# One attention head's scores at a later place among the block products, query transposes ahead of the output projection, and one query chunk in another PSUM bank

## The chip, the cores and the metric

The kernel runs on one core of one Trainium2 chip. The time is the device time of one execution in microseconds (us), taken as the median of several runs. All data are 32-bit floats.

## The reference, cut to what matters

The reference is a cross-attention with two kinds of context rows. There are 8 batches. Each has 112 query rows of 320 channels (`x`) and 375 context rows of 512 channels; the last 4 of those are "prompt" rows and the other 371 are "text" rows. There are 20 heads of 16 channels.

```
q = x @ W_q ; k = text @ W_k ; v = text @ W_v          (per head)
p = softmax(q k^T / 4)                                  112 x 371 per head
text_out = p v
qsem = l2norm(p @ text)                                 112 x 512 per head
fused = q k_ip^T / 4 + 0.5 * qsem @ l2norm(prompts)^T   112 x 4 per head
out = (text_out + softmax(fused) * mask @ v_ip) @ W_out + b_out + x
```

The norm of `p @ text` is the costly part. The kernel never forms the 512 wide product: with G = text text^T (371 x 371, the same for all heads of a batch) the squared norm of a row is p G p^T, so one product of `p` with the triangle of G, a multiplication by `p` and a sum give it. The columns for `p v`, the row sum of `p` and the prompt products are set beside G, so that one chain of matmuls yields all of them.

## The kernel before, in words

**Tiling.** A batch `b` is worked in five steps `g` = 0 to 4 of four heads `a` = 0 to 3 each, so there are 40 steps (b, g). One head lies on 32 of the 128 partitions: head `a` of a step uses partitions 32a to 32a+31. I call these 32 rows of TensorE's array **strip a**. Four matmuls on four strips can be under way together.

**Products of a step** (`multiplied`, L510 to L531). A step has 12 blocks `j` of 32 context rows. In each block every head has one matmul (L523) from its strip: the transposed probabilities of that block against the rows of G and of the values in the tile `u`. Only the upper triangle is multiplied, so the blocks get narrower: 392 columns in block 0, 360 in block 1, and so on by 32 down to 40 in block 11. Each head adds up in a PSUM bank of its own (`ps_qd`, four banks). A matmul of 32-bit floats is two passes in the trace, each with a weight load and a matmul record: 40 steps x 48 matmuls x 2 = 3840 records on L523.

**Scores** (`scores`, L476). While a step's products run, the scores of the step two ahead (`LEAD = 2`) are made for its four heads: one matmul of 371 columns each, on strip `a`, between the blocks. A score goes to one of the two banks of the pool `ps_sc`, taken in turn. `probabilities` then takes the row maximum on VectorE (L489), the exponential on ScalarE (L493), and issues on SyncE's queue the DMA that lays the probabilities of the head out for the transposition (L496). The main loop sets the places by hand:

```
at = {0: (0, 1), 4: (2, 3)}.get(j, ())
```

After block 0 come the scores of heads 0 and 1, after block 4 those of heads 2 and 3. As there are two banks, head 2's score needs head 0's exponential to be done, and head 3's needs head 1's. After block 2 VectorE transposes the coming step's probabilities (`transposed`, L504).

**After the blocks of a step** come `reduced` (ScalarE copies L536, VectorE multiply and sum L538), the GpSimd copies of the next step's values into `u` (`placed`, L445), and then in `between` (L665) the projections of the next batch: `gram` (L362) in step 0, `values` (L409) and `keys` (L393) in steps 1 to 3, and in step 4 the transposes of the context of batch b+2 (`transposed_context`, L339, copies L349), the output projection of batch b-1 (fourth piece of `finish`, L633, with its addition L640 on VectorE) and, in steps (1, 4), (3, 4) and (5, 4) alone, the queries of the coming batches (`project_queries`, L269): two batches at a time, but one in (5, 4).

**`project_queries`** has six pieces: three transposes of chunks of `x` (L281, copied by ScalarE, L284) and three chunks of `x W_q` (L289), each read by VectorE (L298, two readings, or one for the last chunk) and by ScalarE (L301) after VectorE.

**PSUM banks.** `ps_qd` has four, `ps_sc` two, and `ps_mm` two for everything else. `bank(name, spare=True)` takes a bank of `ps_sc` in place of one of `ps_mm`. Before the change these use it: the third chunk of the context (`ps_c`, b > 1), the output projection `ps_o` (all but the last batch), and the first transposed chunk of `x` (`ps_x`).

**Order.** The instructions of TensorE, SyncE and VectorE run in the order in which the program emits them; ScalarE's and GpSimd's are set by the framework's scheduler.

Of the kernel before, what the change touches and what calls it, by code (L numbers as in the profile page):

```python
# [20 lines left out]
def kernel(  # L21
# [58 lines left out]
    def bank(name, spare=False):  # L80

        if spare:
            return ps_sc.tile([P, 512], F32, tag="sc", name=name)
        return ps_mm.tile([P, 512], F32, tag="mm", name=name)
# [21 lines left out]
    FULL = C // P  # L106
# [162 lines left out]
    def project_queries(bs):  # L269
        n = len(bs)  # L270
        xT = work.tile([P, NC, 2 * S], F32, tag="xT", name=f"xT_{bs[0]}", bufs=1)
        qT = work.tile([P, NC, 2 * S], F32, tag="qT", name=f"qT_{bs[0]}", bufs=2)
        qm = work.tile([P, NC, 2, 2 * S], F32, tag="qm", name=f"qm_{bs[0]}", bufs=2)
        for j, b in enumerate(bs):
            queries[b] = (qT, qm, j)
        nc.gpsimd.memset(xT[REST:, FULL, :], 0.0)
        for i in range(NC):
            cn = min(P, C - i * P)
            ps = bank(f"ps_x_{bs[0]}_{i}", spare=bs[0] > 1 and i == 0)
            for j, b in enumerate(bs):  # L280
                nc.tensor.transpose(  # L281
                    ps[:cn, j * S : (j + 1) * S], x_sb[:, b, i * P : i * P + cn], ident[:S, :S]
                )
            nc.scalar.copy(xT[:cn, i, : n * S], ps[:cn, : n * S])  # L284
            yield
        for i in range(NC):
            ps = bank(f"ps_q_{bs[0]}_{i}")
            for j in range(NC):
                nc.tensor.matmul(  # L289
                    ps[:, : n * S],  # L290
                    wq_sb[:, j, i * P : (i + 1) * P],
                    xT[:, j, : n * S],
                    start=(j == 0),
                    stop=(j == NC - 1),
                )

            for r in range(2 if i < FULL else 1):
                nc.vector.tensor_scalar_mul(  # L298
                    qm[:, i, r, : n * S], ps[:, : n * S], emask[:, r : r + 1]
                )  # L300
            nc.scalar.copy(qT[:, i, : n * S], ps[:, : n * S])  # L301
            yield
# [8 lines left out]
    def begin(b):  # L311
        s = st[b] = dict(ct=loaded.pop(b))
        s["ctxT"] = work.tile([P, NE, TP], F32, tag="ctxT", name=f"ctxT_{b}")
        nc.gpsimd.memset(s["ctxT"][:, :, T:], 0.0)
        s["kT"] = work.tile([P, NC, TT], F32, tag="kT", name=f"kT_{b}")
        s["ud"] = dram.tile([P, GCOL[NT]], F32, tag="ud", name=f"ud_{b}")
        s["vext"] = work.tile([P, NT, GROUP, NG, D], F32, tag="vext", name=f"vext_{b}", bufs=1)
        s["vd"] = dram.tile([TP, C], F32, tag="vd", name=f"vd_{b}")
        s["u"] = work.tile([P, UCOL], F32, tag="u", name=f"u_{b}")
        s["vr"] = work.tile([P, BLK, NG, D], F32, tag="vr", name=f"vr_{b}")  # L320
        s["ipl"] = work.tile([S, H, NIP], F32, tag="ipl", name=f"ipl_{b}")
        s["ss"] = work.tile([S, H], F32, tag="ss", name=f"ss_{b}")
        s["pvs"] = work.tile([S, H, VW], F32, tag="pvs", name=f"pvs_{b}")
        s["vip"] = work.tile([S, NIP, H, D], F32, tag="vipb", name=f"vip_{b}")
# [6 lines left out]
    def transposed_context(b):  # L331
        begin(b)
        s = st[b]
        ct, ctxT = s["ct"], s["ctxT"]
        for c in range(NT):
            rows = min(P, TT - c * P)
            ps = bank(f"ps_c_{b}_{c}", spare=b > 1 and c == 2)
            for e in range(NE):
                nc.tensor.transpose(  # L339
                    ps[:, e * P : e * P + rows],  # L340
                    ct[:rows, c, e * P : (e + 1) * P],
                    ident[:rows, :rows],
                )
            o = ctxT[:, :, c * P : c * P + rows]
            i = ps.rearrange("p (e t) -> p e t", t=P)[:, :, :rows]
            if c % 2 and b < 1:
                nc.vector.tensor_copy(o, i)
            else:
                nc.scalar.copy(o, i)  # L349
            yield  # L350

    def gram(b):

        ctxT = st[b]["ctxT"]

        nc.gpsimd.tensor_copy(ctxT[:, :, TT:T], ipnT[:, :, b * NIP : (b + 1) * NIP])
        for c in range(NT):
            t0 = c * P
            k = min(P, TT - t0)
            ps = bank(f"ps_g_{b}_{c}")  # L360
            for e in range(NE):
                nc.tensor.matmul(  # L362
                    ps[:, : T - t0],
                    ctxT[:, e, t0 : t0 + P],
                    ctxT[:, e, t0:T],
                    start=(e == 0),
                    stop=(e == NE - 1),
                )
            g = ug[:, GCOL[c] : GCOL[c] + T - t0]
            nc.scalar.mul(g, ps[:, : T - t0], 2.0)  # L370
            nc.gpsimd.tensor_tensor(g[:, :k], g[:, :k], half[:, :k], ALU.mult)  # L371
            yield
# [127 lines left out]
    def transposed(b, g):  # L500

        xg = x_ring[(b * NG + g) % NX]
        xT = work.tile([P, BLK, P], F32, tag="xgT", name=f"xgT_{b}_{g}")
        nc.vector.transpose(  # L504
            xT.rearrange("p j (k q) -> p q j k", q=QN),
            xg.rearrange("p q (j k) -> p q j k", k=RG),
        )
        st[b]["xT", g] = xT
# [149 lines left out]
    def run(key, make, pieces=1):  # L658

        if key not in gens:  # L660
            gens[key] = make()
        for _ in range(pieces):
            next(gens[key], None)

    def between(b, g):  # L665

        nb = b + 1
        new = nb < B
        later = [bs for bs in pairs if bs[0] == (nb if b == 0 else nb + 1)]
        if g == 0:  # L670
            if b == 0:
                run(("pp",), None)
            if new:
                run(("g", nb), lambda: gram(nb), 3)
            if b > 0:
                run(("f", b - 1), lambda: finish(b - 1))
        if g == 1:
            if new:
                run(("v", nb), lambda: values(nb), 2)
            run(("t", b), lambda: prompt_logits(b))  # L680
            if b > 0:
                run(("f", b - 1), None)
        if g == 2 and new:
            run(("v", nb), None)
            run(("k", nb), lambda: keys(nb))
        if g == 3:
            if new:
                run(("k", nb), None, 2)
            if b > 0:
                run(("f", b - 1), None)  # L690
        if g == 4:
            if nb + 1 < B:
                run(("c", nb + 1), lambda: transposed_context(nb + 1), 3)
            if b > 0:
                run(("f", b - 1), None)
        if b == 0 and g in (1, 2) or b > 0 and g == 4:
            for bs in later:
                run(("q", bs[0]), lambda: project_queries(bs), 3 if b == 0 else 6)

    prompts = normalised_prompts()  # L700
    context = transposed_context(0)
# [42 lines left out]
    for n, (b, g) in enumerate(steps):  # L744
        coming = steps[n + LEAD] if n + LEAD < len(steps) else None
        for j, _ in enumerate(multiplied(b, g)):
            at = {0: (0, 1), 4: (2, 3)}.get(j, ())
            for a in at if coming else ():
                scores(*coming, a)
                probabilities(*coming, a)  # L750
            if j == 2 and n + 1 < len(steps):
                transposed(*steps[n + 1])
        reduced(b, g)
        if n + 1 < len(steps):
            placed(*steps[n + 1])
        new = b + 1 < B
        if g == 0 and b > 1:
            run(("f", b - 2), None)
        if new:
            if g == 1:  # L760
                gram_to_dram(b + 1)
                load_next(b + 2)
            elif g == 2:
                gram_to_groups(b + 1, (0, 1))
            elif g == 3:
                gram_to_groups(b + 1, (2,))
                values_to_dram(b + 1, nc.sync)
        if g == 1 and b == 0:
            run(("pp",), None)
        if g == 2:  # L770
            prompt_values(b)
        between(b, g)
        if g == 3 and new:
            values_to_groups(b + 1, nc.sync)
        if g == 3 and not new:

            first = finish(b, (0, FULL * HC))
            next(first)
            next(first)
# [46 lines left out]
```

## Time and profile before

| | |
|---|---|
| median of 3 runs | 498.68 us (497.80 to 499.25) |
| the profiled execution | 498.01 us |
| its span, first to last instruction | 496.2 us |
| TensorE busy in the span | 468.3 us (94%) |
| VectorE, ScalarE, GpSimd busy | 321.1, 180.1, 105.9 us |
| mean granted TensorE clock | 0.972 |

The page of the profile gives busy times by engine, the chain of work that ended last, and groups of instructions by line. Beside it I read the timeline (instructions in order of time, neighbours of one line merged), the waits, and the single records of the trace where the timeline merges too much. In a line of the timeline the columns are start, duration, engine, line and operation, the tiles (out<-in), the shape, the number of records, and in brackets the idle time before the first and what ended it. PE is TensorE's matmuls, PEld its weight loads, DVE is VectorE, ACT ScalarE, POOL GpSimd, SPq SyncE's queue.

### The profile page before, as it was taken

What the parts mean: (1) busy time and instruction counts of PE and PEld (TensorE: products, weight loads), DVE (VectorE), ACT (ScalarE), POOL (GpSimd) and SP (SyncE); (2) the same over time, 40 slices, a digit from 0 to 9 for tenths busy, and PEclk for the clock granted to TensorE, in tenths of its full rate; (3) what the DMA queues carried; (4) which work ended last, traced back from release to release, by engine and by line L of the source; (5) the groups of instructions that cost most, each with busy time, mean ns of one, the idle gap of its engine ahead of it and who ended that gap; (6) DMA issues with size and microseconds to landing.
All of it is one profiled execution on the core that took longest, in us unless ns stands there. A gap on an engine that the chain in (4) does not pass through costs nothing.

```text
span 496.2 us, 12853 instructions
## 1 busy us (share of the span) xinstructions
PE 468.3 (94%) x5106; PEld 361.8 (73%) x5106; DVE 321.1 (65%) x692; ACT 180.1 (36%) x505; POOL 105.9 (21%) x245
## 2 busy tenths in 40 slices
PE   6999999999999999999999999999999999987963
PEld 3657777788777787788778787788777887766751
DVE  3045456687765775687756776687756776678862
ACT  2253232235334352335324342335324432243232
POOL 4301200002501124012501124012501232011540
PEclk9997999999999999999999999999999999998895
DMA  7588447542595236942595236842595227732300
GB/s 217 157 198 237 100 152 163 156 114 63 154 228 153 58 95 172 210 121 67 163 229 142 67 98 171 199 116 76 171 220 140 67 87 162 195 101 78 101 13 12
DMA packets 61075, 67.24 MB, mean 136 GB/s; under 512 B 22128, under 2 KB 56192, under 8 KB 61016
## 3 DMA queue, kind: packets, MB, share of 16 engines
q1 hardware_dynamic: 60096, 65.32, 50.3%
q10 hardware_dynamic: 920, 1.11, 0.8%
q8 instruction: 40, 0.66, 0.6%
q14 instruction: 19, 0.16, 0.1%
HBM read 31.65 MB, written 8.17 MB: 80 GB/s over the span
## 4 chain that ended last, share of the span: by engine, by line
PE 84%; DVE 5%; ACT 3%; DMA 2%; POOL 2%; issue 2%; SPq 1%; POOLq 0%; ACTq 0%; DVEq 0%
PE ps_qd L523 37%; PE ps_k L393 11%; PE ps_v L409 11%; PE ps_g L362 9%; PE ps_s L476 7%; PE ps_q L289 2%; PE ps_c L339 2%; PE ps_o L633 2%; DVE junk L538 1%; POOL wv L606 1%; DMA vr<-vd 1%; DVE qm L298 1%; PE ps_kip L237 1%; PE ps_ip L456 1%; DMA ip_sb<-in_ctx_dram 1%
## 5 line engine op out<-in xcount | busy, mean ns | idle before, releaser
L523 PE MATMUL ps_qd<-u,xgT 32*112 32x296 f32 (+11 forms) x3840 | 244.4, 365 | 3.5 <-POOL u L445 1.4
L523 PEld LDWEIGHTS ps_qd<-u,xgT 32*112 32x112 f32 x3840 | 196.8, 174 | 33.6 <-issue 7.3
L493 ACT ACTIVATE p<-ps_s,nmx 112x371 f32<-112x371 f32 x160 | 82.3, 568 | 159.8 <-DVE nmx L489 141.6
L489 DVE TENSOR_REDUCE nmx<-ps_s 112x1 f32<-112x371 f32 x160 | 77.4, 528 | 76.0 <-PE ps_s L476 74.7
L504 DVE STREAM_TRANSPOSE xgT<-xg 128x1536 f32<-128x1536 f32 x40 | 118.9, 2971 | 5.2 <-DMA xg<-p 5.2
L538 DVE CUSTOM_DVE_ANT_0 junk<-ps_qd,p 112x371 f32<-112x371 f32 x160 | 87.1, 544 | 45.3 <-ACT pvs L536 28.0
L476 PE MATMUL ps_s<-kT,qm 32*112 32x371 f32 x320 | 75.0, 496 | 2.8 <-ACT p L493 2.2
L445 POOL COPY u<-vr 128x64 f32<-128x64 f32 x120 | 26.6, 238 | 224.8 <-PE ps_qd L523 161.5
L393 PE MATMUL ps_k<-ctxT,wk_sb 128*128 128x371 f32 x192 | 63.6, 480 | 0.0
L409 PE MATMUL ps_v<-wv_sb,ctxT 128*128 128x320 f32 x192 | 55.6, 440 | 0.0
L393 PEld LDWEIGHTS ps_k<-ctxT,wk_sb 128*128 128x128 f32 x192 | 35.7, 190 | 21.7 <-issue 1.1
L476 PEld LDWEIGHTS ps_s<-kT,qm 32*112 32x112 f32 x320 | 36.8, 173 | 15.8 <-ACT kT L400 3.2
L362 PE MATMUL ps_g<-ctxT 128*128 128x375 f32 (+2 forms) x192 | 45.3, 394 | 0.7 <-issue 0.7
L409 PEld LDWEIGHTS ps_v<-wv_sb,ctxT 128*128 128x128 f32 x192 | 35.2, 190 | 13.5
L362 PEld LDWEIGHTS ps_g<-ctxT 128*128 128x128 f32 x192 | 33.4, 197 | 12.3 <-issue 3.8
L400 ACT COPY kT<-ps_k 128x371 f32<-128x371 f32 x24 | 11.3, 469 | 41.4 <-PE ps_k L393 41.3
L606 POOL TENSOR_TENSOR wv<-vip,w 112x1280 f32<-112x1280 f32 (+1 forms) x8 | 19.2, 2404 | 31.8 <-DVE w L604 31.8
L298 DVE TENSOR_SCALAR qm<-ps_q,emask 128x224 f32<-128x224 f32 (+1 forms) x25 | 9.2, 400 | 24.2 <-PE ps_q L289 24.0
L416 ACT COPY vext<-ps_v 128x320 f32<-128x320 f32 x24 | 10.2, 427 | 33.5 <-PE ps_v L409 33.5
L371 POOL TENSOR_TENSOR ug<-ug,half 128x128 f32<-128x128 f32 (+1 forms) x24 | 11.3, 472 | 41.6 <-ACT ug L370 41.6
L536 ACT COPY pvs<-ps_qd 112x21 f32<-112x21 f32 x160 | 16.5, 200 | 6.9 <-PE ps_qd L523 6.9
L289 PE MATMUL ps_q<-xT,wq_sb 128*128 128x224 f32 (+1 forms) x90 | 16.8, 332 | 1.9 <-ACT xT L284 0.9
(95 smaller groups left out, 272.4 us busy)
## 6 DMA issues: line engine op xcount, KB each, us to landing
xg<-p SPq DMA_DIRECT2D x160, 162.3 KB
u<-ud SPq DMA_DIRECT2D x32, 188.0 KB
vip<-vipd SPq DMA_DIRECT2D x8, 560.0 KB
ct<-in_ctx_dram SPq DMA_DIRECT2D x16, 256.0 KB
u<-ud SPq DMA_DIRECT2D x32, 124.0 KB
vr<-vd SPq DMA_DIRECT2D x32, 120.0 KB
vd<-vext SPq DMA_DIRECT2D x7, 480.0 KB
ud<-ug SPq DMA_DIRECT2D x7, 372.0 KB
```

The costliest lines, as they stand in the source:

```text
L289: nc.tensor.matmul(ps[:, : n * S], wq_sb[:, j, i * P : (i + 1) * P], xT[:, j, : n * S], start=(j == 0), stop=(j == NC - 1),)
L362: nc.tensor.matmul(ps[:, : T - t0], ctxT[:, e, t0 : t0 + P], ctxT[:, e, t0:T], start=(e == 0), stop=(e == NE - 1),)
L393: nc.tensor.matmul(ps[:, :TT], wk_sb[:, e, i * P : (i + 1) * P], s["ctxT"][:, e, :TT], start=(e == 0), stop=(e == NE - 1),)
L409: nc.tensor.matmul(ps[:, :C], ctxT[:, e, c * P : (c + 1) * P], wv_sb[:, e, :], start=(e == 0), stop=(e == NE - 1),)
L445: nc.gpsimd.tensor_copy(region(b, c)[:, :, UV - c * P :], s["vr"][:, c * QN : (c + 1) * QN, g, :])
L476: nc.tensor.matmul(ps[:S, :TT], qm[a * RG : (a + 1) * RG, i, r, j * S : (j + 1) * S], s["kT"][a * RG : (a + 1) * RG, i, :], start=True, st ...
L489: nc.vector.tensor_reduce(nmx, ps[:S, :TT], AX.X, ALU.max, negate=True)
L493: nc.scalar.activation(p, ps[:S, :TT], AF.Exp, bias=nmx)
L504: nc.vector.transpose(xT.rearrange("p j (k q) -> p q j k", q=QN), xg.rearrange("p q (j k) -> p q j k", k=RG),)
L523: nc.tensor.matmul(banks[a][:S, j * RG : UW], xT[a * RG : (a + 1) * RG, j, :S], region(b, c)[a * RG : (a + 1) * RG, q, q * RG :], start=(j ...
L538: nc.vector.tensor_tensor_reduce(out=junk, in0=ps[:S, :TT], in1=s["p", g][:, a, :], scale=1.0, scalar=0.0, op0=ALU.mult, op1=ALU.add, accu ...
L606: eng.tensor_tensor(wv, s["vip"][:, :, part], w.rearrange("p h n -> p n h").unsqueeze(3).to_broadcast([S, NIP, n, D]), ALU.mult,)
```

## The change

Four edits, all in the order of work and the choice of banks; no arithmetic changes.

1. Head 3's score (with its maximum, exponential and DMA) is emitted after block 6 in place of block 4. Head 2's stays after block 4.
2. In step 4 of batches 1, 3 and 5 the three transposes of `x` are emitted after the context's transposes and ahead of the output projection; before, they came after it.
3. The three chunks of `x W_q` stay after the output projection (three pieces there in place of six).
4. The third chunk of `x W_q` takes a bank of `ps_sc` in place of one of `ps_mm`, where the first batch of the pair is above 1 (so in the same three steps).

```
         for i in range(NC):
-            ps = bank(f"ps_q_{bs[0]}_{i}")
+            ps = bank(f"ps_q_{bs[0]}_{i}", spare=bs[0] > 1 and i == FULL)
...
         if g == 4:
             if nb + 1 < B:
                 run(("c", nb + 1), lambda: transposed_context(nb + 1), 3)
+            for bs in later if b > 0 else ():
+                run(("q", bs[0]), lambda: project_queries(bs), 3)
             if b > 0:
                 run(("f", b - 1), None)
         if b == 0 and g in (1, 2) or b > 0 and g == 4:
             for bs in later:
-                run(("q", bs[0]), lambda: project_queries(bs), 3 if b == 0 else 6)
+                run(("q", bs[0]), lambda: project_queries(bs), 3)
...
-            at = {0: (0, 1), 4: (2, 3)}.get(j, ())
+            at = {0: (0, 1), 4: (2,), 6: (3,)}.get(j, ())
```

`later` holds the pair of batches whose queries are due; `FULL` is 2.

More of the change, by code (lines that the diff above doesn't have):

```diff
@@ L286, in project_queries @@
         for i in range(NC):
-            ps = bank(f"ps_q_{bs[0]}_{i}")
+            ps = bank(f"ps_q_{bs[0]}_{i}", spare=bs[0] > 1 and i == FULL)
             for j in range(NC):
@@ L693, in between @@
                 run(("c", nb + 1), lambda: transposed_context(nb + 1), 3)
+            for bs in later if b > 0 else ():
+                run(("q", bs[0]), lambda: project_queries(bs), 3)
             if b > 0:
@@ L697, in between @@
             for bs in later:
-                run(("q", bs[0]), lambda: project_queries(bs), 3 if b == 0 else 6)
+                run(("q", bs[0]), lambda: project_queries(bs), 3)
     prompts = normalised_prompts()
@@ L746 @@
         for j, _ in enumerate(multiplied(b, g)):
-            at = {0: (0, 1), 4: (2, 3)}.get(j, ())
+            at = {0: (0, 1), 4: (2,), 6: (3,)}.get(j, ())
             for a in at if coming else ():
```

## The prediction

> **What bounds the kernel.** I read the page first, then the chain, then the timeline of one step and of one stage with queries.
>
> ```profile
> span 496.2 us, 12853 instructions
> ...
> PE   6999999999999999999999999999999999987963
> ...
> PE 84%; DVE 5%; ACT 3%; DMA 2%; POOL 2%; issue 2%; SPq 1%; POOLq 0%; ACTq 0%; DVEq 0%
> ```
>
> TensorE is busy in every slice up to the last batch, and the chain that ended last is TensorE's for 84%. So an edit is worth what it does to TensorE's own order; VectorE and ScalarE count only where TensorE waits for them. Step (3, 4) is typical; its matmuls:
>
> ```profile
> 261.23 0.93 PE L523 MATMUL ps_qd<-u,xgT 32*112 32x392 f32 x8
> 261.98 0.48 PE L476 MATMUL ps_s<-kT,qm 32*112 32x371 f32 x2
> 262.00 0.56 PE L523 MATMUL ps_qd<-u,xgT 32*112 32x360 f32 x2
> ...
> 264.31 0.47 PE L476 MATMUL ps_s<-kT,qm 32*112 32x371 f32 x1
> 264.48 0.39 PE L523 MATMUL ps_qd<-u,xgT 32*112 32x264 f32 x2
> 264.51 0.58 PE L476 MATMUL ps_s<-kT,qm 32*112 32x371 f32 x2
> ```
>
> Here the reader is to see two things. While strips 0 and 1 do their scores (261.98), strips 2 and 3 already start block 1 (262.00). And head 2's score starts at 264.31, head 3's only at 264.51, because its bank is held by head 1's exponential, which ends at 263.43 + 1.03 = 264.46:
>
> ```profile
> 263.43 1.03 ACT L493 ACTIVATE p<-ps_s,nmx 112x371 f32<-112x371 f32 x2 [1.57 <-DVE nmx L489]
> ```
>
> The list of waits shows 2.9 us in two waits for this line, because the other strips keep the engine busy meanwhile. The single records show it in nearly every step.
>
> **The strips, from single records of this step** (times from its start, 261.23; which strip a record is on is inferred from the order). A pass of 371 columns takes 0.31 us (264.310 to 264.621), one of 200 columns 0.17. Strip 3 is last: its final pass starts at 5.66, those of the other strips by 5.38, and the next stage follows at 5.86. Its loss at the score: 0.20 waiting, and 0.09 because the second weight load could not be fetched ahead. What would follow if the wait only vanished is seen in step (3, 0), where the exponentials are early: from head 2's score to the next stage 2.52 us there, 2.78 here. So the prize is 0.26 us a step.
>
> But a strip cannot run far ahead. In this step the first weight loads of blocks 8, 9 and 10 on the leading strips are at 265.624, 265.962, 266.247, and strip 3's first passes of blocks 6, 7 and 8 start at 265.620, 265.958, 266.243: each time 4 ns before. Loads are handed out in order, and at most about three passes wait on one strip.
>
> **Edit 1, step by step.** Head 2's score stays, so strip 2 starts block 5 at 3.70 as now. Strip 3 without its score does block 5 early, but block 6 must be handed out behind strip 2's block 6, thus not before 3.70. A load not fetched ahead costs 0.095 (265.962 to 266.144 is 0.182, of which a pass of 104 columns is 0.087): strip 3 begins block 6 at 3.80. Two passes of 200 columns, 0.34: 4.14. The score, 0.62: block 7 at 4.76. Now it begins block 7 at 265.958, that is 4.73. **The score no longer waits for its bank, and strip 3 idles as long for its turn: +0.03 us a step.** Bounds where this is not seen in the trace: -0.29 (all that the wait costs) to +0.62 (the whole score laid bare). I take +0.03, nearest to the records of strip 3 itself.
>
> In 28 steps of batches 0 to 6 (all but the seven with g = 0) this is 28 x 0.03 = 0.8. In (0, 1) and (0, 2) the wait is 0.05 shorter: +0.1. Where head 3's score does not wait today, the split is paid in full: in (3, 0) strip 2 starts block 5 at 4.18, so block 7 on strip 3 comes at 4.18 + 0.10 + 0.34 + 0.62 = 5.24 against 4.94 now, +0.3; the same in (5, 0) and (0, 0): together +0.9. In (1, 0), whose strips start one after another over 2 us, nothing.
>
> What lies behind it: VectorE.
>
> ```profile
> 262.80 0.99 DVE L489 TENSOR_REDUCE nmx<-ps_s 112x1 f32<-112x371 f32 x2 [3.31 <-PE ps_s L476]
> 263.71 2.96 DVE L504 STREAM_TRANSPOSE xgT<-xg 128x1536 f32<-128x1536 f32 x1
> 266.50 0.95 DVE L489 TENSOR_REDUCE nmx<-ps_s 112x1 f32<-112x371 f32 x2
> ```
>
> Head 3's maximum comes second after the transposition, at 266.9. The moved score ends at about 261.23 + 4.76 + 0.17 = 266.2. So the transposition hides the delay with 0.7 us to spare; the exponential, the DMA on SyncE's queue (nothing is issued there between blocks 4 and 6) and the next transposition keep their times. Without that cover each microsecond would delay `reduced`.
>
> **Edits 2 to 4**, three times. The stage after step (3, 4):
>
> ```profile
> 268.42 1.78 PE L633 MATMUL ps_o<-wo_sb,aT 128*112 128x320 f32 x6
> 270.03 0.74 PE L281 MATMUL ps_x<-ident,x_sb 112*128 112x112 f32 x6
> 271.07 4.09 PE L289 MATMUL ps_q<-xT,wq_sb 128*128 128x224 f32 x18 [0.30 <-ACT xT L284]
> 275.09 0.60 PE L523 MATMUL ps_qd<-u,xgT 32*112 32x392 f32 x4
> ```
>
> Two gaps go: about 0.46 before the first query matmul (ScalarE's copies of `xT`), about 0.31 before the third chunk (its bank is read until 273.70). What is late next is the copies of the context:
>
> ```profile
> 268.22 1.57 ACT L349 COPY ctxT<-ps_c 128x512 f32<-128x512 f32 x3
> ```
>
> They end at 268.85, 269.34 and 269.78. The transposes of `x` now come at 268.42 and need the `ps_mm` banks of the first two; `ps_o` now takes the `ps_sc` bank of the third, where before it took the other. So `ps_o` starts at about 269.83 + 0.10; six matmuls at 0.27 bring the queries to 271.54 (with their load in; now 271.17), 18 at 0.189 end where the next step starts, about 275.03. **Gain 0.06 us, not 0.77.** In (5, 4) the queries are half as wide, its gaps smaller: by the same addition from its copies (end 380.83) the last matmul starts at 384.49 against 384.32, a loss of 0.17. Sum: -0.12 + 0.17 = +0.05. GpSimd's clearing of `xT` (0.28) passes no GpSimd work that anyone awaits; no DMA is passed on SyncE's queue.
>
> **The wait added by edit 4.** With two more banks of `ps_sc` in turn, head 1's score in the next step takes the bank of the third query chunk. That is read last of all:
>
> ```profile
> 275.68 0.35 ACT L301 COPY qT<-ps_q 128x224 f32<-128x224 f32 x1 [0.84 <-DVE qm L298]
> ```
>
> This copy ends 0.95 after the step's start, with the shift about 0.94; head 1's score now starts at 0.76. Waiting, with its load, until about 1.09 holds back 0.33, and behind it all loads of block 1 are queued, strips 2 and 3 too. So (2, 0) and (4, 0) pay 0.33 + 0.03, (6, 0) with its shorter copy about 0.13: +0.85.
>
> **Last batch.** TensorE is not its bound (steps are 8.6, 14.0, 8.6 us long there): 0, between -0.4 and +0.5.
>
> **Sum:** 0.8 + 0.1 + 0.9 + 0.05 + 0.85 = +2.7 us. The profiled execution took 498.01 (span 496.2 and 1.8 around it): 500.7. It lies 0.67 below the median shown, so for the median **501.4**. Own range of this case, with 0.00 to 0.06 in the 28 steps, half to all of the other terms, and the last batch: 499.8 to 503.
>
> **A rule weighed.** The records show a lead of one block. The Trainium skill, page "TensorE: Matmul & The Clock Gate", section "The mechanism" of its part on packing, states a 64-deep window from which weight loads for another row group are pulled ahead. By it strip 3 would run on freely, the 0.26 would be gained 28 times, and the sum would be some 7 us below zero. The same section has matmuls start strictly in order; here block 1 on strips 2 and 3 starts at 262.00, and on strips 0 and 1, earlier in the program, at 262.61. The measurement decides against both.
>
> **Rivals.**
> - *Faster.* Strip 3 may run two blocks ahead once it alone leads. For it: the limit is seen only with two or three strips leading. Against: three loads within 4 ns. It gives 28 x (-0.26) = -7.3, and with the query terms about -6.5: 492. It decides as soon as strip 3 begins block 6 by 3.54 rather than 3.80.
> - *No change.* Head 1's wait fails to come (ScalarE reads the third chunk before the scores are due), and the g = 0 steps swallow the split. For it: ScalarE is idle around 275. Against: it waits for VectorE there. 0.8 + 0.1 + part of 0.9: about 499.4.
> - *Much slower.* The other strips cannot fill the time of a lone score in the narrow blocks: 0.2 more in each step, 5.6: 507. Against: after 265.6 the leading strips already wait for strip 3 today.
>
> **How the numbers follow.** This kernel's measurement tells 0.3%, 1.5 us, from no change. Forecast 0.64, no change 0.18, faster 0.12, much slower 0.06. The forecast's case lies almost all above 500.2, so slower 0.69, same 0.19, faster 0.12. The range leaves out the faster and the much slower case: 498.4 to 503.8.
>
> **What would show it.** In a changed step (3, 4): head 3's score at 4.0 to 4.2 after the start with no wait, the next stage again at 5.86 to 5.92; in (3, 0) at 6.3 to 6.4, now 6.07; in (4, 0) head 1's score at 1.0 to 1.1 and the end at 6.2; `ps_o` at 269.9 relative to the same step. If the next stage comes at 5.6, the limit on the lead is wrong and so is the forecast.

## The result, and the profile after

The changed kernel takes 501.31 us (median of 7 runs, 500.32 to 503.48) where the kernel before takes 498.63 in the same series (7 runs, 496.49 to 500.07): ratio 1.0070, 95% interval [1.0043, 1.0098]. The quotient of the two medians is 1.0054, inside that interval. The kernel is slower by 0.4% to 1.0%. The profiled execution of the changed kernel took 503.48 us, 5.5 more than the one of before: about twice the 2.7 between the medians, so a part of what the two profiles differ by is not the change.

The page of the changed kernel (span; TensorE in 40 slices; the chain by engine):

```profile
span 501.7 us, 12853 instructions
...
PE   5989999999999999999999999999999999997963
...
PE 84%; DVE 7%; ACT 4%; issue 2%; DMA 1%; POOL 1%; POOLq 0%; DVEq 0%; ACTq 0%
```

TensorE is still busy in every slice up to the last batch and still has 84% of the chain. Its timeline in step (3, 4), which now starts at 264.14:

```profile
264.14 0.93 PE L523 MATMUL ps_qd<-u,xgT 32*112 32x392 f32 x8
...
267.22 0.47 PE L476 MATMUL ps_s<-kT,qm 32*112 32x371 f32 x1
...
267.53 0.47 PE L476 MATMUL ps_s<-kT,qm 32*112 32x371 f32 x1
267.62 0.95 PE L523 MATMUL ps_qd<-u,xgT 32*112 32x232 f32 x13
268.28 0.47 PE L476 MATMUL ps_s<-kT,qm 32*112 32x371 f32 x1
...
270.04 0.33 PE L339 MATMUL ps_c<-ident,ct 128*128 128x128 f32 x1
```

The reader is to see the two passes of head 2's score at 267.22 and 267.53 (3.08 and 3.39 after the start, as before), then head 3's alone at 268.28, which is 4.14 after the start and waits for nothing; and the next stage at 270.04, which is 5.89 after the start where before it was 5.86. The wait for the bank has gone, and the step is 0.03 us longer. The single records say why (strips inferred from the order): strip 3 has done block 5 at 267.71, the first weight load of its block 6 comes at 267.850, 4 ns after strip 2 starts its block 5 at 267.846, and the pass itself runs from 267.945. Strip 3 stands idle for 0.24 us there. And it lost 0.09 already at block 5, whose load comes at 267.227, 4 ns after head 2's score starts at 267.223, so that it could not be fetched ahead. Together 0.33; before, strip 3 lost 0.29 at its score.

VectorE behind it, in the same step:

```profile
265.71 0.99 DVE L489 TENSOR_REDUCE nmx<-ps_s 112x1 f32<-112x371 f32 x2 [3.36 <-PE ps_s L476]
266.62 2.95 DVE L504 STREAM_TRANSPOSE xgT<-xg 128x1536 f32<-128x1536 f32 x1
269.42 0.93 DVE L489 TENSOR_REDUCE nmx<-ps_s 112x1 f32<-112x371 f32 x2
```

The late score ends at 269.06. Head 2's maximum starts at 269.42, behind the transposition, and head 3's follows at once with no idle time in the line. So the cover held.

The stage behind this step, TensorE from the context's transposes to the second block of step (4, 0):

```profile
270.04 1.49 PE L339 MATMUL ps_c<-ident,ct 128*128 128x128 f32 x12
271.37 1.31 PE L281 MATMUL ps_x<-ident,x_sb 112*128 112x112 f32 x6
272.74 1.87 PE L633 MATMUL ps_o<-wo_sb,aT 128*112 128x320 f32 x6
274.44 3.57 PE L289 MATMUL ps_q<-xT,wq_sb 128*128 128x224 f32 x18
277.94 0.93 PE L523 MATMUL ps_qd<-u,xgT 32*112 32x392 f32 x8
278.69 0.80 PE L476 MATMUL ps_s<-kT,qm 32*112 32x371 f32 x2
278.95 0.56 PE L523 MATMUL ps_qd<-u,xgT 32*112 32x360 f32 x2
```

The 18 query matmuls take 3.57 us where they took 4.09, but they start 10.30 us after the step's start where they started at 9.84. What holds them are ScalarE's copies of the context, the second line here (ScalarE's timeline of the same stretch):

```profile
269.93 1.03 ACT L493 ACTIVATE p<-ps_s,nmx 112x371 f32<-112x371 f32 x2 [2.56 <-DVE nmx L489]
...
271.12 1.57 ACT L349 COPY ctxT<-ps_c 128x512 f32<-128x512 f32 x3
...
278.54 0.35 ACT L301 COPY qT<-ps_q 128x224 f32<-128x224 f32 x1 [0.43 <-DVE qm L298]
```

The copies end at 272.69, and the output projection starts at 272.74. The last line is the read of the third query chunk; it ends at 278.88, and head 1's score of step (4, 0) starts 0.05 later: 0.99 after the start of that step, by the single records, where it was 0.76. Step (4, 0) reaches its next stage at 6.22 in place of 5.86.

**Which part of the profiles' 5.5 us is the change.** I took each step's length from its start to the start of the next. Start to step (0, 0): +1.12. Step (0, 0): +0.61. Steps (0, 1) to (6, 3): +2.46. Step (6, 4): -0.32. Batch 7 up to its last step: +1.51. The rest: +0.07. Step (6, 4) has 8.58 and 8.23 us in two profiles of the kernel before, so its -0.32 says nothing. The first is a DMA, at the head of the chain of waits of the kernel before and of the changed kernel:

```profile
0.74 3.22 DMA ip_sb<-in_ctx_dram
```

```profile
0.74 4.90 DMA ip_sb<-in_ctx_dram
```

The change touches nothing there, and in the second profile of the changed kernel (below) this DMA takes 3.49. Batch 7 is treated with the runs below. The middle, which repeats to 0.03 us in that second profile, is the change.

Step (0, 0) has to be split at head 2's score, since the orders of work differ only behind it. From head 2's score to the next stage it takes 2.49 us in the kernel before and 2.82 in the changed one, so the change costs 0.33 there. What lies ahead of head 2's score took 5.22 and 4.72 in the two profiles of the kernel before and 5.50 in the changed one; the order of work is the same there.

### The profile page after: what moved, and what is told of

Read it like the earlier page. It is cut to its first block, busy times and chain, and to the rows that moved or that the text cites. A ratio compares the mean times of both kernels' runs of the same rounds, so it can differ in the third digit from the quotient of the medians.

```text
span 501.7 us, 12853 instructions
## 1 busy us (share of the span) xinstructions
PE 474.7 (95%) x5106; PEld 368.5 (73%) x5106; DVE 322.5 (64%) x692; ACT 180.0 (36%) x505; POOL 106.0 (21%) x245
## 3 DMA queue, kind: packets, MB, share of 16 engines
q10 hardware_dynamic: 920, 1.11, 0.8%
## 4 chain that ended last, share of the span: by engine, by line
PE 84%; DVE 7%; ACT 4%; issue 2%; DMA 1%; POOL 1%; POOLq 0%; DVEq 0%; ACTq 0%
PE ps_qd L523 36%; PE ps_k L393 12%; PE ps_v L409 11%; PE ps_g L362 9%; PE ps_s L476 7%; PE ps_q L289 3%; DVE xgT L504 3%; PE ps_o L633 2%; DVE nmx L489 1%; PE ps_c L339 1%; ACT p L493 1%; DVE junk L538 1%; DMA ip_sb<-in_ctx_dram 1%; ACT ctxT L349 1%; PE ps_ip L456 1%
## 5 line engine op out<-in xcount | busy, mean ns | idle before, releaser
L523 PE MATMUL ps_qd<-u,xgT 32*112 32x200 f32 (+11 forms) x3840 | 250.3, 369 | 1.9 <-DVE ss L538 1.1
L523 PEld LDWEIGHTS ps_qd<-u,xgT 32*112 32x112 f32 x3840 | 204.1, 174 | 32.3 <-issue 8.3
L476 PE MATMUL ps_s<-kT,qm 32*112 32x371 f32 x320 | 95.6, 487 | 2.8 <-ACT p L493 2.2
L476 PEld LDWEIGHTS ps_s<-kT,qm 32*112 32x112 f32 x320 | 41.5, 175 | 15.1 <-issue 3.8
L339 PE MATMUL ps_c<-ident,ct 128*128 128x128 f32 (+1 forms) x96 | 13.9, 293 | 5.2 <-DMA ct<-in_ctx_dram 5.1
```

The source lines that it names most:

```text
L339: nc.tensor.transpose(ps[:, e * P : e * P + rows], ct[:rows, c, e * P : (e + 1) * P], ident[:rows, :rows],)
L476: nc.tensor.matmul(ps[:S, :TT], qm[a * RG : (a + 1) * RG, i, r, j * S : (j + 1) * S], s["kT"][a * RG : (a + 1) * RG, i, :], start=True, st ...
L523: nc.tensor.matmul(banks[a][:S, j * RG : UW], xT[a * RG : (a + 1) * RG, j, :S], region(b, c)[a * RG : (a + 1) * RG, q, q * RG :], start=(j ...
```

## The experiments

In the table, "step" is the time from the start of a typical step (3, 3) to its next stage; "middle" is the time from step (0, 1) to the start of (6, 4), against the first profile of before; "batch 7" is the time from step (7, 0) to (7, 4) in that profile.

| kernel | median us | ratio, 95% interval | step | (1, 0) whole | middle | batch 7 |
|---|---|---|---|---|---|---|
| before | 498.2 to 498.75 by series | 1 | 5.86 | 12.64 | 0 | 34.27 |
| changed | 501.31 | 1.0070 [1.0043, 1.0098] | 5.89 | 12.64 | +2.46 | 35.78 |
| edit 1 alone | 501.58 | 1.0060 [1.0034, 1.0087] | 5.89 | 12.64 | +1.73 | 36.2 |
| edits 2 to 4 alone | 499.73 | 1.0028 [1.0002, 1.0054] | 5.86 | 12.65 | +0.14 | 34.7 |
| edits 2, 3 alone | 500.68 | 1.0054 [1.0029, 1.0080] | 5.86 | 12.65 | +1.41 | 35.4 |
| head 3 after block 5 | 495.90 | 0.9942 [0.9916, 0.9967] | 5.66 | 14.34 | -3.19 | 37.1 |
| both after block 5 | 495.03 | 0.9931 [0.9908, 0.9954] | 5.62 | 14.34 | -4.07 | 37.0 |
| both after block 6 | 496.18 | 0.9954 [0.9930, 0.9978] | 5.68 | 14.34 | -2.78 | 36.9 |
| head 3 after block 8 | 505.36 | 1.0136 [1.0098, 1.0175] | 6.00 | 12.66 | +4.75 | 36.5 |
| a bank of its own | 492.61 | 0.9885 [0.9856, 0.9914] | 5.57 | 14.34 | -5.06 | 36.3 |
| own bank, block 5 if g = 4 | 493.49 | 0.9905 [0.9871, 0.9939] | 5.57 | 12.64 | -7.09 | 36.8 |

**Theory A** is that of the prediction: a strip leads the others by one block, so a score made alone lays strip 3 bare as its wait for the bank did. The rivals are named in the expectations.

**Edit 1 alone.**

```
-            at = {0: (0, 1), 4: (2, 3)}.get(j, ())
+            at = {0: (0, 1), 4: (2,), 6: (3,)}.get(j, ())
```

> Head 3's score after block 6, nothing else changed. Theory A (a strip can lead by one block only): 28 steps cost 0.03 each, (3, 0) and (5, 0) 0.27 each, (0, 0) 0.3 to 0.6, and (2, 0), (4, 0), (6, 0) now only 0.03 each, as head 1's score has its old bank: in the profile the next stage starts 5.89 after a typical step's start, 6.33 in (3, 0), 5.89 in (4, 0). Sum about +2.0 us, ratio 1.004. Theory B (the lone score is harmless, the query edits with the bank cost the time): the steps as before, 5.86, and within 0.5 us of before. Theory C (the time is lost in the last batch, where the late score delays the maximum on VectorE): steps to (6, 4) sum to nothing, the last batch is over 1 us longer.

Measured: 501.58; steps at 5.89, (3, 0) at 6.33 for 6.07, and (2, 0), (4, 0), (6, 0) at 5.89 like any other. Edit 1 costs by itself, and it is most of the change. That the cost comes from the queries alone (theory B) falls.

**Edits 2 to 4 alone** (the diff of the change without its last part).

> Transposes of x ahead of the output projection and the third query chunk in a bank of the scores; head 3's score stays after block 4. Theory A: the three stages sum to about 0 (-0.08, -0.08, +0.15), head 1's score in (2, 0) and (4, 0) starts at 0.99 in place of 0.76 and the next stage 0.2 to 0.3 later than 5.86, (6, 0) 0.1 later: sum +0.6 us, not to be told from no change. Theory B: +2 to +3 us. If the gaps of 0.46 and 0.31 us in each stage really were gained: -2 us.

Measured: 499.73, middle +0.14. The stages are as in the changed kernel (13.80, 13.80 and 12.42 us for the steps (1, 4), (3, 4), (5, 4) with their stages, before 13.86, 13.85 and 12.28). But head 1's late score costs only 0.04 in (2, 0) and (4, 0), not the 0.2 to 0.3 expected: it pushes head 2's score from 3.08 to 3.40, and head 3's, which had to wait for its bank anyway, follows at 3.41. The scores of step (4, 0), which starts at 275.65 here:

```profile
276.40 0.80 PE L476 MATMUL ps_s<-kT,qm 32*112 32x371 f32 x2
...
279.06 0.48 PE L476 MATMUL ps_s<-kT,qm 32*112 32x371 f32 x2
279.37 0.48 PE L476 MATMUL ps_s<-kT,qm 32*112 32x371 f32 x2
```

The last two lines have two records each, one of head 2 and one of head 3. The two waits lie on top of each other. In the changed kernel, where head 3's wait is gone, the same delay costs 0.36. So 0.59 of the change's +2.46 belongs to no edit alone: 1.73 + 0.14 is 1.87. The median is 1.6 us above that of before, and these steps explain 0.14 of it; the rest is not explained.

**Edits 2 and 3 alone**, without the bank of edit 4.

```
+            for bs in later if b > 0 else ():
+                run(("q", bs[0]), lambda: project_queries(bs), 3)
             if b > 0:
                 run(("f", b - 1), None)
```

> The kernel before with edits 2 and 3 alone: the transposes of x ahead of the output projection, but the third query chunk stays in a bank of ps_mm; scores as before. Theory F (the queries stay late because their transposes and the output projection wait for the context's copies, so edit 4 pays for itself): without edit 4 the third chunk waits again for the first chunk's readers, so the stages behind (1,4) and (3,4) get 0.2 to 0.4 us longer than before, (5,4) 0.5 to 0.7 longer; (2,0), (4,0), (6,0) go back to 5.86; sum +0.9 to +1.5, about 500. Rival (edits 2 and 3 gain by themselves, as their first gap of 0.3 to 0.46 us goes, and edit 4 only adds the wait of head 1's score): stages 0.2 to 0.5 us shorter, sum about -1, 497.6.

TensorE's timeline behind step (3, 4), which starts at 261.92 here:

```profile
269.10 1.36 PE L281 MATMUL ps_x<-ident,x_sb 112*128 112x112 f32 x6
270.52 1.87 PE L633 MATMUL ps_o<-wo_sb,aT 128*112 128x320 f32 x6
272.22 3.98 PE L289 MATMUL ps_q<-xT,wq_sb 128*128 128x224 f32 x18
276.13 0.60 PE L523 MATMUL ps_qd<-u,xgT 32*112 32x392 f32 x4
```

The queries start at 10.30, as late as in the changed kernel, and take 3.98 in place of 3.57, since the third chunk waits again. The stages are longer by 0.37, 0.37 and 0.67; middle +1.41. So the early transposes lose 0.46 us at the queries' start, and edit 4 pays about as much back. Theory F holds. The median's +2.3 us is more than the middle explains; 1.2 of it stands in batch 7 of the profile, which differs by more between two executions of one kernel (see below).

**Head 3's score after block 5.**

```
-            at = {0: (0, 1), 4: (2, 3)}.get(j, ())
+            at = {0: (0, 1), 4: (2,), 5: (3,)}.get(j, ())
```

> As before, but head 3's score after block 5, head 2's after block 4: one block between them in place of two. Theory A: strip 3 goes straight from block 5 to its score without waiting for its turn or its bank; it starts at 3.45 with no wait, and the next stage comes at 5.65 in place of 5.86 in 31 steps; (3, 0) is 0.07 longer. Sum about -6.3 us, ratio 0.987. Rival D (any lone score costs, since the other strips cannot fill its time): as slow as the changed kernel or nearly, ratio 1.00 to 1.01.

**Both scores after block 5** (`{0: (0, 1), 5: (2, 3)}`).

> As before, but the scores of heads 2 and 3 together after block 5. Theory A: no wait for a bank (head 1's exponential ends at 3.23, the scores come at 3.45 or later), both strips start together; the next stage comes at 5.61 in place of 5.86 in 31 steps, 6.1 in (3, 0). Sum about -7.6 us, ratio 0.985. Rival D expects the same from the pair being together, so this run tells only with the one before: A has the two within 1.5 us of each other, D has them 6 or more apart.

Measured: 495.90 and 495.03; steps at 5.66 and 5.62. Alone after block 5, head 3's score came at 3.57 and not at 3.45: 0.09 of that is the load of its block 5, which was not fetched ahead, as in the changed kernel. That any score made alone costs (theory D) falls: one block apart, the two scores still overlap (strip 2 from 3.08 to 3.70, strip 3 from 3.57 to 4.19), and the loss against the pair is 0.04. The size was expected too large for both. Part of it came back in three places: step (1, 0) takes 1.70 us more, (3, 0) and (5, 0) 0.27 more, and the stages with queries give half of the step's gain back.

**Both scores after block 6** (`{0: (0, 1), 6: (2, 3)}`): head 3's score as late as in the changed kernel, but not alone.

> The kernel before with both scores after block 6 in place of block 4: head 3's score stands as late as in the changed kernel, but head 2's stands beside it. Theory A (being alone costs, not being late): both scores at 3.85 to 4.0, the next stage at 5.65 to 5.72 in typical steps, 0.14 to 0.21 earlier than before; (3,0) and (5,0) at 6.3 to 6.4; (1,0) may be 1.7 longer, as with the pair after block 5; sum -2 to -4, about 496. Rival E (being late costs, as the narrow blocks behind cannot fill the time of a score): next stage at 5.89 or later, and 501 or more.

Step (3, 4), which starts at 259.61 here:

```profile
263.53 0.48 PE L476 MATMUL ps_s<-kT,qm 32*112 32x371 f32 x2
...
263.84 0.48 PE L476 MATMUL ps_s<-kT,qm 32*112 32x371 f32 x2
263.96 1.40 PE L523 MATMUL ps_qd<-u,xgT 32*112 32x168 f32 x38
265.29 0.55 PE L339 MATMUL ps_c<-ident,ct 128*128 128x128 f32 x3
```

Each line has two records: both strips do their scores together, at 3.92 and 4.23, and the next stage comes at 5.68. Being late costs little: 5.62 for the pair after block 5, 5.68 after block 6. Being alone as well costs 0.21 more: 5.89.

**Head 3's score alone after block 8** (`{0: (0, 1), 4: (2,), 8: (3,)}`).

> The kernel before with head 3's score alone after block 8, in place of block 4. Theory A (a strip leads by one block at most, so a score made alone, far from another's, is laid bare but for the lead): head 3's score at 4.7 to 4.8 after the step's start, the next stage at 5.97 to 6.02 in typical steps, 0.10 to 0.15 later than before; (3,0) and (5,0) at 6.4 to 6.5; sum +4 to +6, about 503.5. Rival D (lead is not limited in blocks, the loss is the load not fetched ahead, 0.09): next stage as with block 6, 5.89, and 501.5.

Step (3, 4), which starts at 264.07 here:

```profile
267.15 0.47 PE L476 MATMUL ps_s<-kT,qm 32*112 32x371 f32 x1
...
268.83 0.47 PE L476 MATMUL ps_s<-kT,qm 32*112 32x371 f32 x1
...
270.07 0.33 PE L339 MATMUL ps_c<-ident,ct 128*128 128x128 f32 x1
```

The score stands at 4.76, the next stage at 6.00: the further apart, the longer, 5.66, 5.89, 6.00 for blocks 5, 6, 8. The pair after block 8 was not run, so how much of the last 0.11 is lateness stays open. In (3, 0) and (5, 0) I expected 6.4 to 6.5; they stay at 6.33, as with block 6. The price of the split grew there too: from head 2's score to the next stage it is 2.92 where it was 2.82. But head 2's score itself comes 0.11 earlier, at 3.41, as head 1's score waits less after block 0 (it starts at 1.00, not at 1.11). Even this late VectorE's transposition covers the score: the two maxima behind the transposition start 5.28 after the step's start in both kernels.

**A bank of its own for head 3's score**, from `ps_mm`, in the steps g = 0 to 3 of batches 0 to 6; the places stay those of before.

```
+        elif a == 3 and not early and g != 1 and (b < B - 1 or g < 2):
+            ps = bank(f"ps_s_{b}_{g}_{a}")
```

> As before, with both late scores after block 4, but head 3's score takes a bank of the pool for everything else in the steps 0 to 3 of batches 0 to 6, so that it does not wait for head 1's exponential; the next stage needs that bank only at its second matmul group. Theory A: head 3's score starts 0.01 after head 2's, at 3.08, and the next stage at 5.55 in place of 5.86 in 24 steps, with (3, 0) and (5, 0) as before: -7.2 us in the steps. If strip 3's late end had another cause than the wait, the next stage stays at 5.86 and the time too.

Step (3, 3), which starts at 248.02 (two lines more in this kernel, so L478 is the score):

```profile
251.10 0.48 PE L478 MATMUL ps_s<-kT,qm 32*112 32x371 f32 x2
...
251.41 0.48 PE L478 MATMUL ps_s<-kT,qm 32*112 32x371 f32 x2
251.50 2.17 PE L525 MATMUL ps_qd<-u,xgT 32*112 32x232 f32 x56
253.59 0.58 PE L393 MATMUL ps_k<-ctxT,wk_sb 128*128 128x371 f32 x1
```

Now both scores start at 3.08, and the next stage comes at 5.57: 0.29 less than before, all that the prediction had counted for this wait on strip 3 (0.20 and 0.09), and a little more than the prize of 0.26 that it took from (3, 0). The middle is -5.06 and not -7.2, mostly since step (1, 0) took 1.70 more. Removing the wait pays; removing it by splitting the pair does not.

**The own bank, and both scores after block 5 in the steps g = 4**, which the own bank leaves out:

```
+            at = ({0: (0, 1), 5: (2, 3)} if g == 4 else {0: (0, 1), 4: (2, 3)}).get(j, ())
```

> The kernel in which head 3's score has a bank of ps_mm to itself in the steps g = 0 to 3 of batches 0 to 6 (there both scores after block 4), and in the steps g = 4, where no such bank is free, both scores after block 5. Theory A: steps g = 1 to 3 with the next stage at 5.57, as with the own bank alone; steps g = 4 at 5.62 in place of 5.86; so about -1.4 us beyond the own bank alone, 491 to 491.7. Rival G (TensorE's clock, or the copies of the next stage, takes back what a step saves): steps shorter as said, stages behind (x,4) longer by as much, 492.6.

Measured: 493.49; the own bank alone had 492.61 in another series, and the intervals of the two ratios overlap, so the gain of 1.4 that was expected is not shown. The steps do as theory A says, 5.57 and 5.62, but rival G is half right. Step (3, 4) with its stage is 0.13 shorter than before, not 0.24: the context's copies start 7.00 after the step's start and started 6.99 after it before, since they stand behind the exponentials on ScalarE and not behind TensorE. ScalarE in step (3, 4), which starts at 257.37 here:

```profile
263.18 1.03 ACT L495 ACTIVATE p<-ps_s,nmx 112x371 f32<-112x371 f32 x2 [2.58 <-DVE nmx L491]
264.10 0.41 ACT L538 COPY pvs<-ps_qd 112x21 f32<-112x21 f32 x4
264.37 1.57 ACT L349 COPY ctxT<-ps_c 128x512 f32<-128x512 f32 x3
```

In (0, 4) nothing is left. And (3, 0), (5, 0) are 0.21 longer. Without step (1, 0), the middle is 0.3 us shorter than with the own bank alone.

**The same kernels again.** The kernel before, the changed one and the one with both scores after block 5, one profile each.

> The kernel before, profiled a second time, to see what of a profile repeats. If theory C holds (the late score makes the last batch longer), batch 7 takes again 34.3 us from the start of (7, 0) to that of (7, 4), against 35.8 of the changed kernel. If the last batch differs by the phase of the granted clock alone, it comes out 1 us or more away from 34.3 here. The steps of batches 0 to 6 should repeat to 0.02 us: 5.86 to the next stage.

> The changed kernel, profiled a second time. Steps of batches 0 to 6 repeat: 5.89, 6.33 in (3, 0), 6.22 in (4, 0). Theory C: batch 7 again 35.8 to 36 us from (7, 0) to (7, 4); by the clock's phase alone: anywhere from 34 to 37.

> Both late scores after block 5, profiled a second time. In its first profile step (1, 0) took 1.7 us longer than before, with the granted clock at 0.54 for 2.5 us of it, while it is 1.00 there before. If this belongs to the kernel (the core stands half idle at the start of that step in all kernels, but here after a shorter stage), it comes again; if it was the phase of that execution, (1, 0) ends at 12.6 in place of 14.3. The other steps at 5.62 again.

The steps of batches 1 to 6 repeat to 0.03 us, all but (6, 4): 5.86, 5.89 and 5.62. Batch 7 does not. The kernel before took 34.27 us from (7, 0) to (7, 4) in its first profile and 38.56 in its second; the changed kernel 35.78 and 35.76. By stretches of batch 7, in the kernel before (busy time of each engine, then the granted clock, the DMA share and GB/s):

```profile
443.20:457.10 13.90, 9.92 (x124) 7.54 (x119) 10.76 (x28) 6.87 (x18) 1.68 (x6) 0.88 0.29 80
457.10:465.80 8.70, 7.55 (x107) 6.06 (x106) 7.45 (x18) 2.59 (x9) 5.97 (x6) 0.80 0.21 57
```

the same two steps in the changed kernel, and then the whole of batch 7 in the kernel before again:

```profile
447.60:461.70 14.10, 10.49 (x127) 8.33 (x120) 11.02 (x29) 6.94 (x18) 1.77 (x6) 0.81 0.29 81
461.70:469.80 8.10, 8.10 (x106) 6.77 (x106) 6.29 (x13) 1.98 (x5) 6.00 (x6) 0.69 0.18 50
```

```profile
437.00:475.60 38.60, 32.83 (x431) 26.61 (x428) 28.87 (x63) 12.78 (x35) 9.41 (x18) 0.82 0.25 72
```

The clock is low in parts of this batch, and how low differs by execution of one and the same kernel: over the whole batch it is 0.90 in the first profile of before and 0.82 in the second. But the clock does not explain most of the difference in length. Of the 4.3 us between these two profiles 3.0 stand in step (7, 3), where the clock is 1.00 in both (first profile, then second):

```profile
465.80:471.40 5.60, 5.52 (x99) 4.67 (x100) 4.48 (x8) 0.46 (x5) 1.01 (x5) 1.00 0.51 162
464.48:473.13 8.65, 6.71 (x108) 4.99 (x104) 5.28 (x10) 2.65 (x11) 0.94 (x4) 1.00 0.33 107
```

In the second, VectorE's transposition waits 2.6 us for the DMA of the probabilities (0.8 in the first), and TensorE 1.7 for the transposition. That a late score lengthens batch 7 (theory C) is not shown: five profiles whose order of work in batch 7 is that of before (before twice, edits 2 to 4, edits 2 and 3, a bank of its own) range from 34.3 to 38.6, and the two of the changed kernel lie within. An effect of 1 us or so could hide in this.

## Why the prediction was right

1. **The main step held in mechanism and size.** Strip 3 begins block 6 at 3.80 after the start, its score stands at 4.14, the step is +0.03 to +0.04 in all typical steps: all three as worked out. 25 of them give +0.89. (0, 1) and (0, 2): +0.17 together, foreseen 0.16.
2. **(3, 0) and (5, 0)**: +0.27 and +0.28, foreseen 0.3 each. (1, 0): 0, as foreseen. **(0, 0)**: the whole step is +0.61 and +0.63 in the two profiles, but its first part differs by 0.65 among the kernels with the scores of before. From head 2's score on it is 2.49 in all five profiles with head 3's score after block 4 and 2.82 in all three with edit 1: +0.33, foreseen 0.3.
3. **Edits 2 to 4**: stages -0.08, -0.09 and +0.13 beside the step's 0.03 (-0.04, -0.05 and +0.17 together with it), foreseen -0.06, -0.06 and +0.17. The one line of the copies of the context, with the banks followed through, gave this; the two visible gaps, 0.77 us, would have given a gain.
4. **The wait of head 1's score**: +0.36, +0.36 and +0.16 in (2, 0), (4, 0) and (6, 0), foreseen 0.36, 0.36 and 0.13. What the prediction did not see is that this price exists only together with edit 1.
5. **Batch 7** was put at 0. Nothing contradicts it, as the two profiles of before bracket both of after, but nothing shows it either.
6. **The sum**: foreseen 2.4 for the middle and 0.3 for (0, 0); measured +2.46 and +0.33. The medians differ by 2.7; the ratio puts the difference at 2.1 to 4.9. That the median of 501.31 came within 0.1 of the 501.4 foreseen is luck, since single executions of the changed kernel spread over 3.2 us.

Of the rivals, *faster* asked for strip 3 at 3.54 and would have shown 5.6: it showed 3.80 and 5.89. *No change* asked that head 1's wait fail to come: it came. Its 499.4 fits its terms only if counted from the profiled execution, while the other cases are counted from the median; on the median its terms give 499.6 to 500.5, nearer to the forecast than it said. *Much slower* feared that narrow blocks cannot fill the time of a lone score. Not with block 6; with block 8 the step loses 0.14, not the 0.2 it asked for.

The rule weighed there (the Trainium skill, page "TensorE: Matmul & The Clock Gate", section "The mechanism") has a 64-deep window from which loads of other row groups are pulled ahead. Read as the prediction reads it, so that strip 3 runs on freely, head 3's score alone after block 5, 6 or 8 would leave the step's length the same (an estimate from that page). Measured are 5.66, 5.89 and 6.00.

What stays open: what happens in batch 7, and why the medians of most kernels differ from before by about 1 us more than their steps do. The limit of one block is inferred from the times; no record shows a queue.

## What to carry to other kernels

When work on strips of TensorE waits for something, ask what the strip will wait for next: in these traces loads go out in order, so a strip that is freed alone only waits for its turn. Keep matmuls of equal size on neighbouring strips side by side (the same work took 5.57, 5.62 and 5.68 with both scores together after block 4, 5 and 6, and 5.66, 5.89 and 6.00 with head 3's one, two and four blocks behind head 2's), and take a wait away by a free bank rather than by moving the waiting matmul. Before moving transposes ahead of a projection, look which copies free their banks: here it cost 0.37 us a stage until another bank paid for it.

## What the runs showed of the hardware

- Step (1, 0) has two lengths, 12.64 and 14.34 us, and nothing between. The products of that step in the kernel before, in the one with a bank of its own, and in that with the own bank and block 5:

```profile
104.67:112.10 7.43, 7.43 (x105) 5.56 (x105) 6.09 (x11) 2.18 (x6) 0.48 (x2) 1.00 0.33 91
```

```profile
103.68:112.80 9.12, 9.12 (x105) 6.66 (x105) 6.39 (x11) 3.12 (x9) 0.51 (x3) 0.81 0.29 82
```

```profile
103.79:111.20 7.41, 7.41 (x105) 5.62 (x105) 6.06 (x11) 2.19 (x6) 0.47 (x2) 1.00 0.36 102
```

  The same 105 matmuls take 1.7 us longer at a granted clock of 0.81. Both profiles with both scores after block 5 have it, and every kernel that shows it has shorter steps in batch 0, but so has the last one, which keeps its clock. In the kernel with a bank of its own the clock is 0.50 for one stretch:

```profile
106.28:109.69 3.41, 3.41 (x32) 2.45 (x28) 2.80 (x3) 1.03 (x2) 0.00 (x0) 0.50 0.04 11
```

  In all 14 profiles the granted clock changes only at moments that lie a multiple of 3.41 us apart. In the five with the long step such a moment falls 2.5 to 2.8 us after the step's start, and the clock is 0.50 for the 3.41 us that follow. In the other nine it falls 0.2 to 2.1 us after the start, and the clock stays 1.00. In all of them the step begins with 2.0 us in which the products come one strip after another (6 records). So the length goes with where the step's start falls between these moments; no run tested this, and why the clock changes at such a moment or stays is not shown. The Trainium skill, page "TensorE: Matmul & The Clock Gate", section "What's actually happening", has the clock fall after an idle window of some 3.4 us. The length of the window agrees with the traces, 3.41 us. That the window is idle is not what they show: the longest idle time of TensorE within 16 us of the step's start is 0.5 us.
- A weight load that was not fetched ahead cost 0.09 to 0.10 us; in the changed kernel it stands at the start of block 6 on strip 3 (load 267.850, pass 267.945).
- Two profiles of the kernel before agree to 0.03 us in the steps of batches 1 to 6, all but (6, 4), which differs by 0.35. They differ by 4.3 us in batch 7 and by 1.7 us up to the first step. So a difference of two spans says little here, and the sum over the steps says much.
